# A spectral and matrix-root layer on one Trainium2 core: transfers and norms kept in the order of the source

## The chip, the cores and the metric

The kernel runs on one core of a Trainium2 chip. The core has five engines that matter here: TensorE (PE) multiplies matrices, and its weight loads have a row of their own (PEld); VectorE (DVE), ScalarE (ACT) and GpSimd (POOL) work elementwise; SyncE (SP) only issues transfers. Transfers (DMA) are issued here from SP's queue and from ACT's. Each engine has its own stream of instructions. The metric is the time of one execution in device microseconds (us), as the median of several runs; lower is better.

## What is computed

The input is 32 images of 32 channels of 128 x 128 values in float32. Two layers follow each other, each behind a group norm and each added to its input:

```
x = x + root(group_norm(x))     # per image and channel: Newton-Schulz iteration on A = the 128 x 128 plane
x = x + conv(group_norm(x))     # 2-D FFT, low modes mixed across channels by weights, inverse FFT

def root(A):                    # 5 steps
    norm = sqrt(sum(A * A));  Y = A / norm;  Z = I
    repeat 5:  T = 0.5 * (3 I - Z Y);  Y = Y T;  Z = T Z
    return Y * sqrt(norm)
```

The first layer takes nearly all of the matrix products: chains of 128 x 128 products for each of 1,024 planes. The second needs, for each image, products with small cosine and sine tables, a product over channels for each of the kept modes, and the way back.

## The kernel before, in words

**Sets and lanes.** Work of the first layer is cut into 256 sets; a set (b, g) is four channels of image b. `newton` (L296) is the chain of products of one set, written as a generator with twelve working steps and an end. Four lanes run four sets at a time, and one round of the main loop (L618 to L653) takes each lane one step on; lane i starts three rounds after lane i - 1. So a lane takes a new set every 13 rounds, and an image, eight sets, takes 26 rounds.

**Staging.** Before a set starts it is staged (`stage` L578, `staged` L260): POOL makes `x`, the normed transposed plane (L266, four instructions), ACT makes `b`, a scaled plane, in place (L274, four instructions), and POOL makes `r` from it (L282). Each time a lane takes a set, the next set is staged, and behind that the loads of the set two further on are issued from ACT's queue (`fetch` L254: L256 loads `b`, with 6 buffers, and L257 loads `xt`, with 14). Inside the chain, PE writes products to psum banks; DVE evacuates them as `v`, `w`, `q`, `t` (L237) and as the result `xt` (L317); ACT evacuates others as `y`, `m`, `mb`, `t` (L229, L231); POOL makes a second `r` from `mb` (L306).

**Statistics.** The norm of an image's first layer needs the statistics of the whole image, which `prep` (L156) makes for image b + 1 while image b is being staged: eight loads `xs` on SP (L163, two buffers), four statistics instructions on DVE for each (L171), and then a chain of small operations to `made[b]`. It takes one step a round.

**Forward.** Each finished pair of sets is transformed (`forward` L322): a product with a table (L326), a copy `sw` (L328), two stores of the result to the scratch tensor `mid` on SP (L330), statistics for the second norm (L332, L342), transposes and copies `u` (L337). After the fourth pair, `spectrum` (L350) ends with `spec` (L392) and its store to `xs` in DRAM (L403).

**Mode products and inverse.** The images fall into two groups, 28 and 4. When a group's spectra are stored, `mode_products` (L409) loads weights `wt` (L417) and spectra `xk` (L421), multiplies (L442), copies to `om` (L452, L454) and stores to `od` (L424), in 32 steps. Then `inverse` (L503) runs for each image: it loads `ob` (L474) and, for each half d of the image, two tiles `yt` of `mid` (L487, seven buffers of 512 KB), multiplies with tables (L524), copies `gt` (L534), multiplies again (L542), adds in place (L547), and stores the tile to `out` (L501). `store(lag)` keeps the last tile back for one step. In the source, the loads of the next half stand right behind the first tile's add of this half. Inverses of the first group are interleaved with the last sets of the first layer; what is left runs after the last set, in the `tail`, where some loads and stores go through ACT's queue.

**What sets the order.** The source above is traced once, and each engine gets its instructions from a scheduler. It keeps the dependencies of data and buffers. Apart from these it may put an instruction ahead of others that the source has before it on the same engine, when by the scheduler's own estimate of times its operands are ready sooner. At run time each queue is worked off in the order that the scheduler gave it.

Of the kernel before, what the change touches and what calls it, by code (L numbers as in the profile page):

```python
# [24 lines left out]
ALU = mybir.AluOpType  # L25
# [31 lines left out]
def conv_preact_kernel(  # L57
# [79 lines left out]
    def moments(st, tag):  # L137
# [15 lines left out]
        nc.vector.scalar_tensor_tensor(d, d, 64.0, f[:, :, :, 2], ALU.mult, ALU.add)  # L153
        return ms, nm, d

    def prep(b, made):  # L156

        st = small.tile([P, C, 6], F32, tag="a_st", name=f"a_st{b}")
        tiles = []

        def load(i):
            t = stp.tile([P, 4, P], F32, tag="xs", name=f"xs{b}_{i}")
            nc.sync.dma_start(out=t, in_=xt_in[b, :, 4 * i : 4 * i + 4, :])  # L163
            tiles.append(t)

        load(0)
        load(1)
        yield
        for i in range(C // 4):
            for c in range(4):  # L170
                nc.vector.bn_stats(st[:, 4 * i + c, :], tiles[i][:, c, :])  # L171
            if i + 2 < C // 4:
                load(i + 2)
            yield
        _, nm, d = moments(st, "a")
        q = small.tile([P, C], F32, tag="a_qs", name=f"a_qs{b}")
        nc.vector.tensor_reduce(
            q, d.rearrange("p g (c e) -> p (g c) e", e=2), AX.X, ALU.add
        )
        pq = bank()[:, 0, 0:C]  # L180
        nc.tensor.matmul(pq, avg_mean, q, start=True, stop=True)

        v = small.tile([P, C + G], F32, tag="a_v", name=f"a_v{b}")
        nc.vector.tensor_scalar_mul(v[:, 0:C], pq, -512 / (P * P))
        yield
        vg = small.tile([P, G], F32, tag="a_vg", name=f"a_vg{b}")
        nc.vector.tensor_reduce(
            vg, v[:, 0:C].rearrange("p (g c) -> p g c", c=2), AX.X, ALU.add
        )
        nc.vector.tensor_scalar(v[:, C:], vg, 0.5, EPS, ALU.mult, ALU.add)  # L190
        s = root(v, C + G, "a_r")
        inv = small.tile([P, C + G], F32, tag="a_inv", name=f"a_inv{b}")
        nc.vector.reciprocal(inv, s)
        yield

        sc = small.tile([P, C], F32, tag="a_sc", name=f"a_sc{b}")
        nc.vector.tensor_scalar_mul(sc, inv[:, 0:C], 1.0 / P)  # L197
        n = small.tile([P, G, 2], F32, tag="a_n", name=f"a_n{b}")
        nc.vector.tensor_tensor(
            n,  # L200
            s[:, 0:C].rearrange("p (g c) -> p g c", c=2),
            inv[:, C:, None].to_broadcast([P, G, 2]),
            ALU.mult,
        )
        nn = small.tile([P, C], F32, tag="a_nn", name=f"a_nn{b}")
        nc.vector.tensor_scalar_mul(
            nn, n.rearrange("p g c -> p (g c)"), P * (1.5 / EYE) ** 2
        )
        sn = root(nn, C, "a_t")

        scr = small.tile([P, C], F32, tag="a_scr", name=f"a_scr{b}")
        nc.vector.tensor_scalar_mul(scr, sc, QR * QS)
        off = small.tile([P, G, 2], F32, tag="a_off", name=f"a_off{b}")
        nc.vector.tensor_tensor(
            off,
            scr.rearrange("p (g c) -> p g c", c=2),
            nm[:, :, None].to_broadcast([P, G, 2]),
            ALU.mult,
        )
        made[b] = (nm, sc, sn, scr, off.rearrange("p g c -> p (g c)"))  # L220
        yield
# [31 lines left out]

    def fetch(b, g):  # L254
        xt, t = four("xt", 14), four("b", 6)
        nc.scalar.dma_start(out=t, in_=x[b, :, 4 * g : 4 * g + 4, :])  # L256
        nc.scalar.dma_start(out=xt, in_=xt_in[b, :, 4 * g : 4 * g + 4, :])  # L257
        raw[b, g] = xt, t

    def staged(b, g, nm, sc, sn, scr, off):  # L260

        chans = range(4 * g, 4 * g + 4)
        m = four("x", 4)
        xt, mb = raw.pop((b, g))
        for j, c in enumerate(chans):
            nc.gpsimd.tensor_scalar(  # L266
                m[:, j, :],
                xt[:, j, :],
                nm[:, c // 2 : c // 2 + 1],
                sc[:, c : c + 1],  # L270
                ALU.add,
                ALU.mult,
            )
            nc.scalar.activation(  # L274
                mb[:, j, :],
                mb[:, j, :],
                AF.Identity,
                bias=off[:, c : c + 1],
                scale=scr[:, c : c + 1],
            )  # L280
        r = four("r", 4)
        nc.gpsimd.tensor_tensor(r, mb, eye, ALU.add)  # L282
        return xt, m, mb, r
# [38 lines left out]
    def forward(b, q, u, st, pair):  # L322
# [4 lines left out]
        sw = sp.tile([P, 4, P], F32, tag="sw", name="sw", bufs=2)  # L327
        nc.scalar.copy(sw, ps)  # L328
        for i, xt in enumerate(pair):
            nc.sync.dma_start(out=mid[b][:, 8 * q + 4 * i : 8 * q + 4 * i + 4, :], in_=xt)  # L330
        for j in range(4):
            nc.vector.bn_stats(st[:, 8 * q + j, :], pair[0][:, j, :])  # L332
        yield
# [16 lines left out]
    def spectrum(b, u, st):  # L350
# [3 lines left out]
        for s in range(2):  # L354
# [45 lines left out]
        )  # L400
        yield
        i, j = where[b]
        nc.sync.dma_start(  # L403
            out=xs[i][:, :, j, :].rearrange("k p m -> p k m"),
            in_=spec.rearrange("p k q t -> p k (q t)"),
        )
        yield

    def mode_products(i):  # L409
# [3 lines left out]
        def load(step):  # L413
            kk, h = divmod(step, 2)
            for l4 in range(4):
                rows = slice(32 * l4, 32 * l4 + 32)
                (nc.scalar if tail and l4 % 2 else nc.sync).dma_start(  # L417
                    out=wts[step % len(wts)][rows, l4], in_=wk[kk, h, rows]
                )
            if not h:  # L420
                nc.sync.dma_start(out=xks[kk % len(xks)][:, 0:n, :], in_=xs[i][kk])  # L421

        def store(kk, om):
            nc.sync.dma_start(  # L424
                out=od[i][:, kk].rearrange("e q b x -> (q b) e x"),
                in_=om.rearrange("p (e o) l -> p e (o l)", e=2),
            )

        for step in range(len(wts)):
            load(step)  # L430
# [38 lines left out]
    def load_products(b):  # L469
        if b < B and b not in obs:  # L470
            g, n = where[b]
            pool, bufs = (ends[0], 4) if ends and last(b) else (inv, 2)
            obs[b] = pool.tile([P, 16, L], F32, tag="ob", name=f"ob{b}", bufs=bufs)
            nc.sync.dma_start(  # L474
                out=obs[b], in_=od[g][:, :, :, n].rearrange("e k q x -> (e k q) x")
            )

    def load_input(b, d):

        if (b, d) in yts:  # L480
            return
        yts[b, d] = []
        for e in range(2):
            o = 16 * e + 8 * d
            pool, tag, bufs = (ends[0], "late", 10) if ends and last(b) else (inv, "yt", 7)
            y = pool.tile([P, 8, P], F32, tag=tag, name=f"yt{b}_{o}", bufs=bufs)
            nc.sync.dma_start(out=y, in_=mid[b][:, o : o + 8, :])  # L487
            yts[b, d].append(y)

    def last(b):  # L490
# [7 lines left out]
    def store(lag):  # L498
        while len(stores) > lag:
            b, o, y = stores.pop(0)  # L500
            (nc.scalar if tail else nc.sync).dma_start(out=out[b, :, o : o + 8, :], in_=y)  # L501

    def inverse(b):  # L503

# [198 lines left out]
```

## Time and profile before

The time before is 3503.25 us, the median of 3 runs (3502.49 to 3504.72). The profiled execution has a span of 3507.2 us and a mean granted PE clock of 0.979.

| Engine | busy us | share of the span |
|---|---|---|
| PE | 3329.1 | 95% |
| PEld | 2980.6 | 85% |
| DVE | 2276.4 | 65% |
| ACT | 1461.1 | 42% |
| POOL | 1102.1 | 31% |

The transfers move 466.93 MB. The largest groups of issues are the loads `b`, `xt` and `xs` and the stores `mid` (256 issues each, 256 KB), the loads `yt` (128, 512 KB) and the stores `out` (128, 512 KB).

How to read the lines that follow: "L274" is line 274 of the kernel; `b<-in_x` names what is written and what is read, with buffer numbers left out; in a wait, the engine and line left of the arrow stood idle until what is right of it was done; "SPq" and "ACTq" are the queues that issue transfers. In a timeline a line gives the start, the duration, the engine, the line and the operation, how many instructions of the kind are merged, and in brackets the idle time of the engine just before and what ended it.

### The profile page before, as it was taken

What the parts mean: (1) busy time and instruction counts of PE and PEld (TensorE: products, weight loads), DVE (VectorE), ACT (ScalarE), POOL (GpSimd) and SP (SyncE); (2) the same over time, 40 slices, a digit from 0 to 9 for tenths busy, and PEclk for the clock granted to TensorE, in tenths of its full rate; (3) what the DMA queues carried; (4) which work ended last, traced back from release to release, by engine and by line L of the source; (5) the groups of instructions that cost most, each with busy time, mean ns of one, the idle gap of its engine ahead of it and who ended that gap; (6) DMA issues with size and microseconds to landing.
All of it is one profiled execution on the core that took longest, in us unless ns stands there. A gap on an engine that the chain in (4) does not pass through costs nothing.

```text
span 3507.2 us, 80642 instructions
## 1 busy us (share of the span) xinstructions
PE 3329.1 (95%) x31936; PEld 2980.6 (85%) x31936; DVE 2276.4 (65%) x6391; ACT 1461.1 (42%) x3025; POOL 1102.1 (31%) x1552
## 2 busy tenths in 40 slices
PE   5999999999999999999999999999999999899765
PEld 5999999999999999999999999999999886667433
DVE  6766666777776767676666666777676546556333
ACT  3444444444444444444444444444444443323111
POOL 4333333333333333333333333333333221111100
PEclk9999999999999999999999999999999999999877
DMA  5333223332333233322322333233323667867897
GB/s 186 125 110 96 88 88 94 97 97 91 97 97 96 92 96 98 93 93 90 95 90 86 94 97 97 91 97 97 95 94 100 201 208 250 268 226 247 281 317 271
DMA packets 281097, 466.93 MB, mean 133 GB/s; under 512 B 92176, under 2 KB 94224, under 8 KB 280720
## 3 DMA queue, kind: packets, MB, share of 16 engines
q1 hardware_dynamic: 198448, 303.40, 27.0%
q10 hardware_dynamic: 82272, 158.37, 14.1%
q8 instruction: 252, 4.13, 0.5%
q14 instruction: 125, 1.02, 0.1%
HBM read 302.28 MB, written 159.38 MB: 132 GB/s over the span
## 4 chain that ended last, share of the span: by engine, by line
PE 67%; DVE 15%; DMA 11%; issue 6%; POOL 1%; SPq 0%; ACT 0%; ACTq 0%; DVEq 0%; POOLq 0%
PE ps L243 51%; PE ps L249 9%; DMA xs<-in_xt 6%; PE ps L326 3%; DVE a_st L171 2%; PE ps L542 2%; DVE q L237 2%; DMA out<-yt 2%; DVE xt L317 2%; DVE w L237 1%; PE ps L442 1%; DMA yt<-mid 1%; DVE a_sc L197 1%; PE ps L524 1%; DVE b_st L342 1%
## 5 line engine op out<-in xcount | busy, mean ns | idle before, releaser
L306 POOL TENSOR_TENSOR r<-mb,eye 128x512 f32<-128x512 f32 x256 | 326.0, 1273 | 1562.4 <-ACT mb L231 1528.1
L266 POOL TENSOR_SCALAR x<-xt,a_nm,a_sc 128x128 f32<-128x128 f32 x1024 | 446.0, 453 | 599.7 <-PE ps L243 568.1
L243 PE MATMUL ps<-w,v 128*128 128x128 f32 x4096 | 549.1, 277 | 5.7 <-DVE w L237 5.5
L243 PE MATMUL ps<-y,q 128*128 128x128 f32 x4096 | 545.2, 276 | 0.0
L243 PEld LDWEIGHTS ps<-w,v 128*128 128x128 f32 x4096 | 500.2, 192 | 18.7 <-issue 8.7
L243 PEld LDWEIGHTS ps<-y,q 128*128 128x128 f32 x4096 | 500.2, 192 | 8.2 <-issue 8.1
L274 ACT ACTIVATE b<-b,a_off,a_scr 128x128 f32<-128x128 f32 x1024 | 430.0, 486 | 178.3 <-DMA b<-in_x 173.9
L237 DVE SCALAR_TENSOR_TENSOR w<-ps,r 128x512 f32<-128x512 f32 x512 | 350.3, 684 | 129.4 <-PE ps L249 124.3
L237 DVE SCALAR_TENSOR_TENSOR v<-ps,m 128x512 f32<-128x512 f32 x256 | 176.1, 688 | 355.4 <-PE ps L243 337.6
L229 ACT COPY y<-ps 128x512 f32<-128x512 f32 x512 | 299.9, 586 | 256.3 <-PE ps L243 248.5
L237 DVE SCALAR_TENSOR_TENSOR q<-ps,eye 128x512 f32<-128x512 f32 x512 | 347.5, 679 | 25.5 <-PE ps L243 9.9
L237 DVE SCALAR_TENSOR_TENSOR v<-ps,x 128x512 f32<-128x512 f32 x256 | 176.5, 689 | 254.1 <-PE ps L243 254.1
L282 POOL TENSOR_TENSOR r<-b,eye 128x512 f32<-128x512 f32 x256 | 326.2, 1275 | 0.0
L317 DVE SCALAR_TENSOR_TENSOR xt<-ps,a_t_s,xt 128x128 f32<-128x128 f32 x1024 | 292.7, 341 | 42.5 <-PE ps L243 42.4
L249 PE MATMUL ps<-ident,v 128*128 128x128 f32 x2048 | 317.9, 276 | 0.8 <-DVE v L237 0.8
L229 ACT COPY m<-ps 128x512 f32<-128x512 f32 x256 | 149.3, 583 | 401.1 <-PE ps L243 388.6
L243 PEld LDWEIGHTS ps<-m,q 128*128 128x128 f32 x2048 | 249.8, 192 | 70.4 <-DVE q L237 37.0
L243 PEld LDWEIGHTS ps<-x,q 128*128 128x128 f32 x2048 | 249.6, 192 | 57.1 <-DVE v L237 50.2
L547 DVE TENSOR_TENSOR yt<-ps,yt 128x512 f32<-128x512 f32 x256 | 164.5, 684 | 205.0 <-PE ps L542 190.2
L171 DVE BATCH_NORM_STATS2 a_st<-xs 128x6 f32<-128x128 f32 x1024 | 237.0, 278 | 84.6 <-DMA xs<-in_xt 84.0
L243 PE MATMUL ps<-m,q 128*128 128x128 f32 x2048 | 283.6, 281 | 7.4 <-DVE q L237 6.4
L243 PE MATMUL ps<-x,q 128*128 128x128 f32 x2048 | 282.5, 281 | 0.8 <-DVE q L237 0.8
(110 smaller groups left out, 5057.9 us busy)
## 6 DMA issues: line engine op xcount, KB each, us to landing
b<-in_x ACTq DMA_DIRECT2D x256, 256.0 KB, 2.9
xt<-in_xt ACTq DMA_DIRECT2D x256, 256.0 KB, 2.9
xs<-in_xt SPq DMA_DIRECT2D x256, 256.0 KB, 2.9
mid<-xt SPq DMA_DIRECT2D x256, 256.0 KB, 2.0
yt<-mid SPq DMA_DIRECT2D x128, 512.0 KB, 5.0
out<-yt SPq DMA_DIRECT2D x90, 512.0 KB, 5.6
out<-yt ACTq DMA_DIRECT2D x38, 512.0 KB, 6.8
od<-om SPq DMA_DIRECT2D x32, 512.0 KB, 3.5
```

The costliest lines, as they stand in the source:

```text
L171: nc.vector.bn_stats(st[:, 4 * i + c, :], tiles[i][:, c, :])
L229: nc.scalar.copy(t, ps)
L237: nc.vector.scalar_tensor_tensor(s, ps, f, t, ALU.mult, ALU.add)
L243: nc.tensor.matmul(ps[:, j, :], lhsT[:, j, :], rhs[:, j, :], start=True, stop=True)
L249: nc.tensor.transpose(ps[:, j, :], t[:, j, :], ident)
L266: nc.gpsimd.tensor_scalar(m[:, j, :], xt[:, j, :], nm[:, c // 2 : c // 2 + 1], sc[:, c : c + 1], ALU.add, ALU.mult,)
L274: nc.scalar.activation(mb[:, j, :], mb[:, j, :], AF.Identity, bias=off[:, c : c + 1], scale=scr[:, c : c + 1],)
L282: nc.gpsimd.tensor_tensor(r, mb, eye, ALU.add)
L306: nc.gpsimd.tensor_tensor(r, mb, eye, ALU.add)
L317: nc.vector.scalar_tensor_tensor(xt[:, j, :], ps[:, j, :], sn[:, c : c + 1], xt[:, j, :], ALU.mult, ALU.add)
L326: nc.tensor.matmul(ps[64 * i : 64 * i + 64], tab[:, T_FW], xt, start=True, stop=True)
L547: nc.vector.tensor_add(y, py[i], y)
```

## The change

Thirteen places are wrapped in `kept`, a helper of the framework. It adds an edge of order, without a wait, from the wrapped instruction to the one that the source has just before it on the same engine. The wrapped instruction then can't be issued ahead of anything that stood before it on that engine; instructions that are not wrapped still can be moved past it. Wrapped are all transfers of the loops (SP's and ACT's) and the two norms of a set (L266 on POOL and L274 on ACT). All operations, buffers and sizes stay as they were. It is for the case in which the scheduler takes an input as landed sooner than it lands, and puts an instruction that needs it ahead of work that could go.

```diff
         nc.vector.scalar_tensor_tensor(d, d, 64.0, f[:, :, :, 2], ALU.mult, ALU.add)
         return ms, nm, d
 
+    kept = tc.keep_in_program_order
+
     def prep(b, made):
 
         st = small.tile([P, C, 6], F32, tag="a_st", name=f"a_st{b}")
...
 
         def load(i):
             t = stp.tile([P, 4, P], F32, tag="xs", name=f"xs{b}_{i}")
-            nc.sync.dma_start(out=t, in_=xt_in[b, :, 4 * i : 4 * i + 4, :])
+            kept(nc.sync.dma_start(out=t, in_=xt_in[b, :, 4 * i : 4 * i + 4, :]))
             tiles.append(t)
 
         load(0)
...
 
     def fetch(b, g):
         xt, t = four("xt", 14), four("b", 6)
-        nc.scalar.dma_start(out=t, in_=x[b, :, 4 * g : 4 * g + 4, :])
-        nc.scalar.dma_start(out=xt, in_=xt_in[b, :, 4 * g : 4 * g + 4, :])
+        kept(nc.scalar.dma_start(out=t, in_=x[b, :, 4 * g : 4 * g + 4, :]))
+        kept(nc.scalar.dma_start(out=xt, in_=xt_in[b, :, 4 * g : 4 * g + 4, :]))
         raw[b, g] = xt, t
 
     def staged(b, g, nm, sc, sn, scr, off):
...
         m = four("x", 4)
         xt, mb = raw.pop((b, g))
         for j, c in enumerate(chans):
-            nc.gpsimd.tensor_scalar(
-                m[:, j, :],
-                xt[:, j, :],
-                nm[:, c // 2 : c // 2 + 1],
-                sc[:, c : c + 1],
-                ALU.add,
-                ALU.mult,
+            kept(
+                nc.gpsimd.tensor_scalar(
+                    m[:, j, :],
+                    xt[:, j, :],
+                    nm[:, c // 2 : c // 2 + 1],
+                    sc[:, c : c + 1],
+                    ALU.add,
+                    ALU.mult,
+                )
             )
-            nc.scalar.activation(
-                mb[:, j, :],
-                mb[:, j, :],
-                AF.Identity,
-                bias=off[:, c : c + 1],
-                scale=scr[:, c : c + 1],
+            kept(
+                nc.scalar.activation(
+                    mb[:, j, :],
+                    mb[:, j, :],
+                    AF.Identity,
+                    bias=off[:, c : c + 1],
+                    scale=scr[:, c : c + 1],
+                )
             )
         r = four("r", 4)
         nc.gpsimd.tensor_tensor(r, mb, eye, ALU.add)
...
         sw = sp.tile([P, 4, P], F32, tag="sw", name="sw", bufs=2)
         nc.scalar.copy(sw, ps)
         for i, xt in enumerate(pair):
-            nc.sync.dma_start(out=mid[b][:, 8 * q + 4 * i : 8 * q + 4 * i + 4, :], in_=xt)
+            kept(nc.sync.dma_start(out=mid[b][:, 8 * q + 4 * i : 8 * q + 4 * i + 4, :], in_=xt))
         for j in range(4):
             nc.vector.bn_stats(st[:, 8 * q + j, :], pair[0][:, j, :])
         yield
...
         )
         yield
         i, j = where[b]
-        nc.sync.dma_start(
+        kept(nc.sync.dma_start(
             out=xs[i][:, :, j, :].rearrange("k p m -> p k m"),
             in_=spec.rearrange("p k q t -> p k (q t)"),
-        )
+        ))
         yield
 
     def mode_products(i):
...
             kk, h = divmod(step, 2)
             for l4 in range(4):
                 rows = slice(32 * l4, 32 * l4 + 32)
-                (nc.scalar if tail and l4 % 2 else nc.sync).dma_start(
+                kept((nc.scalar if tail and l4 % 2 else nc.sync).dma_start(
                     out=wts[step % len(wts)][rows, l4], in_=wk[kk, h, rows]
-                )
+                ))
             if not h:
-                nc.sync.dma_start(out=xks[kk % len(xks)][:, 0:n, :], in_=xs[i][kk])
+                kept(nc.sync.dma_start(out=xks[kk % len(xks)][:, 0:n, :], in_=xs[i][kk]))
 
         def store(kk, om):
-            nc.sync.dma_start(
+            kept(nc.sync.dma_start(
                 out=od[i][:, kk].rearrange("e q b x -> (q b) e x"),
                 in_=om.rearrange("p (e o) l -> p e (o l)", e=2),
-            )
+            ))
 
         for step in range(len(wts)):
             load(step)
...
             g, n = where[b]
             pool, bufs = (ends[0], 4) if ends and last(b) else (inv, 2)
             obs[b] = pool.tile([P, 16, L], F32, tag="ob", name=f"ob{b}", bufs=bufs)
-            nc.sync.dma_start(
+            kept(nc.sync.dma_start(
                 out=obs[b], in_=od[g][:, :, :, n].rearrange("e k q x -> (e k q) x")
-            )
+            ))
 
     def load_input(b, d):
 
...
             o = 16 * e + 8 * d
             pool, tag, bufs = (ends[0], "late", 10) if ends and last(b) else (inv, "yt", 7)
             y = pool.tile([P, 8, P], F32, tag=tag, name=f"yt{b}_{o}", bufs=bufs)
-            nc.sync.dma_start(out=y, in_=mid[b][:, o : o + 8, :])
+            kept(nc.sync.dma_start(out=y, in_=mid[b][:, o : o + 8, :]))
             yts[b, d].append(y)
 
     def last(b):
...
     def store(lag):
         while len(stores) > lag:
             b, o, y = stores.pop(0)
-            (nc.scalar if tail else nc.sync).dma_start(out=out[b, :, o : o + 8, :], in_=y)
+            kept((nc.scalar if tail else nc.sync).dma_start(out=out[b, :, o : o + 8, :], in_=y))
 
     def inverse(b):
 
```

## The prediction

> **What bounds the kernel now.** I read the page's slices first, then the windows, then the waits of each stretch, then the timelines. The slices show three parts: a slow start, a long flat stretch, and an end in which TensorE (PE) empties while DMA fills.
>
> ```profile
> PE   5999999999999999999999999999999999899765
> PEclk9999999999999999999999999999999999999877
> DMA  5333223332333233322322333233323667867897
> ```
>
> The windows put numbers on them (columns: span, busy PE, PEld, DVE, ACT, POOL, granted clock, DMA share, GB/s).
>
> ```profile
> 0.00:100.00 100.00, 60.97 (x473) 57.61 (x474) 64.14 (x241) 36.17 (x80) 39.83 (x63) 1.00 0.58 185
> 1000.00:1500.00 500.00, 496.54 (x4230) 465.44 (x4226) 350.78 (x1032) 229.13 (x477) 181.40 (x256) 1.00 0.31 95
> 2900.00:3000.00 100.00, 88.70 (x1067) 62.75 (x1065) 58.85 (x138) 33.53 (x69) 16.96 (x24) 0.97 0.78 252
> 3000.00:3100.00 100.00, 87.06 (x1092) 62.57 (x1092) 48.78 (x96) 32.16 (x67) 16.97 (x24) 0.92 0.75 250
> 3300.00:3370.00 70.00, 41.51 (x514) 18.79 (x512) 20.38 (x42) 10.06 (x20) 8.83 (x6) 0.70 0.93 321
> ```
>
> From 100 to 2700 us PE is 99% busy, and the timeline shows its groups of eight matmuls back to back, one every 0.89 us (1522.24, 1523.13 and so on). Nothing off PE can shorten that. What can move lies in the start and after 2850 us, where the inverse transforms (L503 to L557) join the last sets. Waits from 2850 to 3230 (total us, times, longest):
>
> ```profile
> ACT b L274 <- DMA b<-in_x: 43.9, 10, 8.5
> PE ps L542 <- ACT gt L534: 18.0, 7, 5.2
> SPq L487 <- DMA out<-yt: 200.5, 67, 8.0
> ```
>
> The first two are one event. ScalarE (ACT) stands at a norm of a set (L274) whose input was issued at 2894.99; the copies `gt` behind it are late, and so is PE:
>
> ```profile
> 2902.16 1.26 ACT L274 ACTIVATE b<-b,a_off,a_scr 128x128 f32<-128x128 f32 x3 [8.54 <-DMA b<-in_x]
> 2904.86 2.08 PE L542 MATMUL ps<-gt,tab 64*128 64x512 f32 x4 [4.39 <-ACT gt L534]
> 2907.77 1.82 PE L243 MATMUL ps<-y,t 128*128 128x128 f32 x8
> ```
>
> Eight matmuls then take 1.82 us instead of 1.06: the clock fell too. The third wait is SyncE's queue (SP). Loads stand ahead of stores there: at 3244.10 a load goes, at 3244.47 two stores, then the queue stands 6 us at the next load, which needs a buffer that a store frees.
>
> ```profile
> 3244.10 0.32 SPq L487 DMA_DIRECT2D yt<-mid  x1
> 3244.47 0.91 SPq L501 DMA_DIRECT2D out<-yt  x2
> 3251.56 0.33 SPq L487 DMA_DIRECT2D yt<-mid  x1
> ```
>
> Stores that are ready wait behind it: image 18's third tile was added by 3232.7 and its store went at 3244.5.
>
> **What the Trainium skill says.** "TensorE: Matmul & The Clock Gate", Architectural detail, says that ACT's and VectorE's (DVE's) queues are strict FIFO; the 8.54 us above and the late copies behind it agree. The same page, Part 1, says that PE falls to half clock after an idle window of about 3.4 us; the 4.39 us gap and the 1.82 us group agree. "DMA: Bandwidth & Descriptors", Issuing engines are not separate DMA queues, says that all queues share the same 16 DMA engines, so reordering gives no bandwidth of its own; here loads land in 2.9 us (median) but in 7 to 12 us when many are out after 3300.
>
> **The change, part by part.** It adds no work. I compared the k-th instruction of each line in the trace with its place in the source. PE's order is already the source's up to 2690 us, except the small matmul L181. The pinned lines run early: L274 by 30 ACT instructions, L257 by 65, L256 by 12 (medians), L266 by 3 on GpSimd (POOL), and the statistics' loads L163 by some 25 SP instructions against the stores L330 around them (an image has 17 of both kinds). The copies on ACT, not pinned, keep their order among themselves.
>
> *Start, -10 us.* ACT now issues 20 input loads in the first 23 us and SP eight weight loads, between the eight loads of image 0's statistics; those land at 6.5 to 24.8. In source order only one set's two loads and the table accompany them. Estimate: first pair at about 6 and 7, then a pair every 3.85 us (0.33 issue + 2.5 landing, as in the quiet stretch from 29 on, + 0.87 statistics + 0.1), so the last statistics end at about 19.4 instead of 25.7: -6. Image 1's statistics no longer stand in the chain of small DVE operations (a 0.53 us wait and several pieces of 0.28): -1. POOL ran L266 of four sets ahead of the first L282, and the first `w` stood for it; in source order L282 follows four L266: -3.
>
> ```profile
> 41.13 0.69 DVE L237 SCALAR_TENSOR_TENSOR w<-ps,r 128x512 f32<-128x512 f32 x1 [3.41 <-POOL r L282]
> ```
>
> *Steady stretch, 0.* An image takes 93.4 us (the same store L330 of images 15 and 16 goes at 1505.02 and 1598.38), and eight sets on four lanes of 13 rounds are 26 rounds: 3.6 us a round. In source order a set's loads stand two stagings, 6.5 rounds or 23 us, ahead of its L274 and land in 2.9, so the 109.5 us of ACT waits for `b` between 200 and 2680 go; PE never felt them. New on ACT is a burst of 4 x 0.48 + 2 x 0.33 = 2.6 us per set. Behind it wait the copies of later lanes; a copy has a round of 3.6 us less 0.9 of matmuls and 0.6 of its own, so about 2 us of slack, and ACT is 46% busy. POOL's L266 and L282 (3.1 us) come a round or more ahead of the next L306. SP's L163 waits for the statistics two tiles back, L330 for adds a round old; behind each stand only loads due two rounds later. Bounds: 0 to +0.3 us per set.
>
> *2850 to 3230, -22 us.* PE's idle time there is 1.3 + 11.3 + 12.9 + 1.3 = 27 us, and the clock's shortfall 3 + 8 + 2 = 13 us, 40 in all. The waits for `b` vanish; those for late psum copies or an inverse's own latency stay. I take a little over half.
>
> *3230 to 3370, -22 us.* Stores go before loads, so the seven `yt` buffers come free sooner. Images 19 to 22 now take 18.1 us each (the same load L487 of images 19 and 23 goes at 3234.7 and 3307.1), for 4.25 MB of tiles; at the 321 GB/s of the next window that is 13.2 us: 4 x 4.9 = 20, of which I take 17, since other transfers share the rate. Then the last image's chain (copy `sw` 3313.7, `spec` 3349.3, its store landing after 12.4 us, 3.2 in the median) loses the weight issues and hoisted input loads ahead of it. But DMA is 93% busy there, and the ten hoisted tiles (5.2 MB, 16 us) only move into the next 95 us, which have 16% free: -5.
>
> *3370 to the end, 0.* SP is in source order there from 3403 on already.
>
> Sum: -10 - 22 - 22 = -54; 3503 - 54 = 3449 us.
>
> **The rivals.** (1) Hidden: the end is bound by bytes, and freed stores only crowd the loads. For it: 93% DMA share from 3300. Against: 75 to 78% before that. Then -10 - 11 = -21: 3482. (2) Slower: the ACT burst, or statistics that now come just in time, delay an evacuation in every round. For it: DVE is 70% busy and its statistics bunch into eight rounds an image. Against: they are bunched more densely now (a load every 1.5 to 2.5 us from 1555 on) and PE does not wait. At 0.3 us on 256 sets +77, less 54: 3526. (3) All of it: -12, -40, -40: 3411.
>
> **How the numbers follow.** Forecast 0.60, hidden 0.20, slower 0.12, all 0.08. The range runs from rival 3 to just above rival 1, 3411 to 3490, and leaves out rival 2. Within 0.2% (3496 to 3510) lie the edges of rivals 1 and 2, 0.04; slower 0.10; faster 0.86.
>
> **What would show it.** First matmul of a set at about 26 instead of 34 us; ACT waits for `b` near zero; PE 99% busy and clock 1.00 from 2900 to 3200; SP waits for `out` far under 200 us; stores within a few us of their adds. I am wrong if PE shows new waits for ACT or DVE between 200 and 2680, or if the inverses' adds (L547) wait for `yt`: those loads landed some 20 us ahead of use from 2900 to 3150 and will be issued one half-image, about 10 us, ahead of it, against 4 to 6 us to land.

## The result and the profile after

| | median us | range us | runs |
|---|---|---|---|
| before | 3502.87 | 3501.16 to 3504.72 | 4 |
| after | 3462.56 | 3458.04 to 3465.06 | 4 |

The ratio is 0.9883, with a 95% interval of 0.9866 to 0.9900: 40 us faster, where 54 us were forecast. The profiled executions lie further apart than the medians (3507.2 and 3456.3 us, 51.0). All stages below are read from one profiled execution of each kernel, so their sizes are good to some 5 to 10 us in the sum, and better where several kernels show the same.

The slices of the kernel after show how the end has changed: PE stays at nine tenths or more up to the 38th slice, where it had begun to give way at the 35th, and DMA is fuller.

```profile
PE   6999999999999999999999999999999999999955
PEclk9999999999999999999999999999999999999977
DMA  3323333333222232333333322233233568898997
```

Windows of the kernel after (columns as before: span, busy PE, PEld, DVE, ACT, POOL, granted clock, DMA share, GB/s). The last two are the stages that take the place of 3300 to 3370 us and of what followed.

```profile
0.00:100.00 100.00, 68.94 (x534) 65.78 (x534) 60.85 (x196) 32.86 (x69) 39.29 (x60) 0.98 0.35 114
1000.00:1500.00 500.00, 495.88 (x4225) 464.83 (x4224) 346.13 (x1004) 228.69 (x476) 183.37 (x258) 1.00 0.31 94
2900.00:3000.00 100.00, 99.24 (x1304) 70.98 (x1303) 62.89 (x150) 37.14 (x76) 20.12 (x29) 0.98 0.91 301
3000.00:3100.00 100.00, 99.56 (x1325) 71.41 (x1323) 62.99 (x125) 36.25 (x74) 20.43 (x28) 1.00 0.91 304
3230.00:3303.00 73.00, 55.21 (x884) 29.66 (x883) 38.36 (x82) 16.66 (x32) 8.90 (x6) 0.91 0.98 351
3303.00:3405.00 102.00, 62.44 (x1239) 43.78 (x1242) 19.56 (x30) 12.00 (x21) 0.00 (x0) 0.71 0.87 282
```

From 2900 to 3100 us PE went from 88 to 99% busy, as the forecast asked for. The waits of 2850 to 3230 us in the kernel after (total us, times, longest) have no line of ACT for `b` any more, and none of SP for `out`; SP now stands at the stores, until the add is done:

```profile
SPq L507 <- DVE yt L553: 142.4, 43, 7.5
ACT gt L540 <- PE ps L530: 66.4, 39, 5.3
```

At the start, DVE makes the first `w` at 32.07 instead of 41.13 us, and does not stand for `r`; what is just ahead of it are statistics of image 1, which were forecast to leave its way:

```profile
31.28 0.87 DVE L173 BATCH_NORM_STATS2 a_st<-xs 128x6 f32<-128x128 f32 x4 [0.49 <-DMA xs<-in_xt]
32.07 0.69 DVE L239 SCALAR_TENSOR_TENSOR w<-ps,r 128x512 f32<-128x512 f32 x1
```

Lines of the changed kernel are shifted: L163 is now L165, L256 and L257 are L258 and L259, L266 and L274 are L269 and L279 (their pins stand in L268 and L278), L330 is L336, L403 is L409, L417, L421 and L424 are L423, L427 and L430, L442 is L448, L474 is L480, L487 is L493, L501 is L507, L547 is L553.

**Where the time went.** The table compares the time of the same instruction in the traces: the end of set 31 (428.5 us before), the end of set 223 (2673.6), the first add of image 0's inverse (2880.2), of image 12's (3118.8), the first and the last matmul of the second group's mode products (3372.2 and 3458.3), and the end. Each cell is the change of one stage against the kernel before, in us; a minus is a gain. The kernels below "after" are the experiments.

| kernel, and what it keeps in order | to set 31 | sets 31 to 223 | to image 0 | images 0 to 12 | to modes of group 2 | modes of group 2 | rest | sum |
|---|---|---|---|---|---|---|---|---|
| after: all | -7.6 | +0.7 | +8.6 | -33.7 | -36.5 | +15.5 | +2.0 | -51.0 |
| e_act: ACT's loads, norms | -3.8 | -17.7 | +0.5 | -8.8 | +9.4 | -0.6 | -1.3 | -22.3 |
| e_sp: all but those | +1.6 | +17.0 | +11.5 | -11.9 | -36.3 | +18.9 | +0.9 | +1.7 |
| e_inv: ob, yt, out | +2.7 | -1.3 | +1.2 | -6.7 | -29.8 | +20.5 | +1.0 | -12.4 |
| e_actinv: both of these | -3.4 | -16.3 | -0.5 | -33.9 | -29.9 | +16.7 | +2.3 | -65.0 |
| e_norms: norms alone | -4.4 | -17.0 | +0.8 | -17.3 | +5.2 | -1.8 | +0.1 | -34.4 |
| e_fetch: ACT's loads alone | -3.6 | -2.8 | -0.6 | -9.6 | +6.9 | +1.6 | -0.3 | -8.4 |
| e_noxs: all but xs | -6.7 | -16.3 | +1.8 | -35.0 | -36.9 | +19.6 | -0.1 | -73.6 |
| e_nomp: all but wt, xk, od | -5.3 | +2.9 | +7.5 | -34.7 | -31.8 | +17.3 | +2.8 | -41.3 |
| e_actyt: e_act and yt | -5.9 | -19.8 | -1.1 | -34.7 | -30.6 | +11.7 | -0.6 | -81.0 |
| e_late: e_actinv, late yt free | -3.4 | -18.3 | -1.3 | -34.4 | -25.7 | +3.3 | -0.7 | -80.5 |
| e_ytlate: e_actyt, late yt free | -6.4 | -16.9 | -1.4 | -34.6 | -26.5 | +8.5 | -0.7 | -78.0 |
| e_noxslate: e_noxs, late yt free | -7.3 | -16.6 | +2.0 | -35.1 | -22.8 | +1.8 | +0.7 | -77.3 |

The whole change is thus a sum of large gains and of three losses (sets 31 to 223 next to e_act, the way to image 0, the modes of group 2), and the experiments are there to name the part behind each.

### The profile page after: what moved, and what is told of

Read it like the earlier page. It is cut to its first block, busy times and chain, and to the rows that moved or that the text cites. A ratio compares the mean times of both kernels' runs of the same rounds, so it can differ in the third digit from the quotient of the medians.

```text
span 3456.3 us, 80446 instructions
## 1 busy us (share of the span) xinstructions
PE 3315.2 (96%) x31936; PEld 2975.0 (86%) x31936; DVE 2264.4 (66%) x6391; ACT 1462.0 (42%) x3025; POOL 1108.4 (32%) x1552
## 3 DMA queue, kind: packets, MB, share of 16 engines
q10 hardware_dynamic: 82272, 158.37, 14.5%
## 4 chain that ended last, share of the span: by engine, by line
PE 83%; DMA 10%; DVE 5%; issue 1%; SPq 1%; ACTq 0%; ACT 0%; DVEq 0%
PE ps L245 62%; PE ps L251 10%; DMA xs<-in_xt 4%; PE ps L332 3%; PE ps L548 3%; PE ps L362 2%; PE ps L530 1%; DVE xt L323 1%; DVE a_st L173 1%; DMA xt<-in_xt 1%; DMA wt_late<-in_wk 1%; PE ps L448 1%; DMA yt<-mid 1%; DMA od<-om 1%; DMA out<-yt 1%; DVE q L239 1%
## 5 line engine op out<-in xcount | busy, mean ns | idle before, releaser
L269 POOL TENSOR_SCALAR x<-xt,a_nm,a_sc 128x128 f32<-128x128 f32 x1024 | 445.6, 449 | 21.7 <-DVE a_n L201 20.1
L279 ACT ACTIVATE b<-b,a_off,a_scr 128x128 f32<-128x128 f32 x1024 | 422.5, 486 | 1.8 <-DMA b<-in_x 1.6
L239 DVE SCALAR_TENSOR_TENSOR q<-ps,eye 128x512 f32<-128x512 f32 x512 | 347.4, 679 | 32.7 <-PE ps L245 19.6
L233 ACT ACTIVATE mb<-ps 128x512 f32<-128x512 f32 x256 | 154.0, 602 | 465.2 <-PE ps L251 463.2
L245 PE MATMUL ps<-m,q 128*128 128x128 f32 x2048 | 282.3, 280 | 16.2 <-DVE q L239 16.1
L245 PE MATMUL ps<-y,t 128*128 128x128 f32 x2048 | 280.2, 277 | 1.3 <-DVE t L239 1.2
```

The source lines that it names most:

```text
L233: nc.scalar.mul(t, ps, f)
L239: nc.vector.scalar_tensor_tensor(s, ps, f, t, ALU.mult, ALU.add)
L245: nc.tensor.matmul(ps[:, j, :], lhsT[:, j, :], rhs[:, j, :], start=True, stop=True)
L269: nc.gpsimd.tensor_scalar(m[:, j, :], xt[:, j, :], nm[:, c // 2 : c // 2 + 1], sc[:, c : c + 1], ALU.add, ALU.mult,)
L279: nc.scalar.activation(mb[:, j, :], mb[:, j, :], AF.Identity, bias=off[:, c : c + 1], scale=scr[:, c : c + 1],)
```

## Experiments

Every kernel is the changed one with some pins taken off. The helper is split in two, and a place that is to be left to the scheduler calls `free`:

```diff
-    kept = tc.keep_in_program_order
+    kept, free = tc.keep_in_program_order, lambda i: i
```

### One part of the change at a time

The working theory was that the two parts gain each for itself and add up: ACT's part (loads and norms) in the start and from 2850 us on, SP's part where stores stand behind loads. Of its rivals, S puts the whole gain on SP's order and A on ACT's.

**e_act**: only L258, L259, L268 and L278 are kept.

```diff
-            kept(nc.sync.dma_start(out=t, in_=xt_in[b, :, 4 * i : 4 * i + 4, :]))
+            free(nc.sync.dma_start(out=t, in_=xt_in[b, :, 4 * i : 4 * i + 4, :]))
...
-            kept(nc.sync.dma_start(out=y, in_=mid[b][:, o : o + 8, :]))
+            free(nc.sync.dma_start(out=y, in_=mid[b][:, o : o + 8, :]))
```

(and so at every other transfer of L336 to L507.)

> Only the set's two loads (L258, L259 in the changed kernel) and its norms (L268 on POOL, L278 on ACT) are kept in order; SP's queue stays free to be moved. Theory (two separate gains, ACT's queue in the start and from 2850 to 3230, SP's after that, less two losses of prefetching): the start gains 6 us, ACT's 44 us of waits for b from 2850 to 3230 go and with them some 25 us, stores still wait behind loads after 3230: about 3475. Rival S (SP's order is the whole gain, the waits for b only mirror crowded transfers): only the start moves, 3496. Rival A (ACT's order is the whole gain, the end is bound by bytes): as the whole change, 3462.

Measured: 3485.51 us, ratio 0.9944 (0.9921 to 0.9967).

**e_sp**: the opposite, every pin but those four places.

```diff
-        kept(nc.scalar.dma_start(out=t, in_=x[b, :, 4 * g : 4 * g + 4, :]))
-        kept(nc.scalar.dma_start(out=xt, in_=xt_in[b, :, 4 * g : 4 * g + 4, :]))
+        free(nc.scalar.dma_start(out=t, in_=x[b, :, 4 * g : 4 * g + 4, :]))
+        free(nc.scalar.dma_start(out=xt, in_=xt_in[b, :, 4 * g : 4 * g + 4, :]))
```

(and so at L268 and L278.)

> All transfers but the set's two loads are kept in order; those and the norms stay free. Theory: ACT's waits for b from 2850 to 3230 stay at some 40 us and so does PE's idle time there; stores go within a few us of their adds and the end gains some 35 us; the lost prefetching costs some 20: about 3488. Rival S: 3462. Rival A: no gain, 3503 or above.

Measured: 3508.97 us, ratio 1.0010 (0.9996 to 1.0024): no gain at all.

**e_inv**: only the transfers of the inverses, `ob` (L480), `yt` (L493) and `out` (L507), are kept; the diff is as for e_act.

> Only the inverse's transfers (ob, yt, out) are kept in order. Theory: the end gains some 35 us as above, the mode products keep their early weights, the first yt tiles are no longer early (+5): about 3478, with the waits for b from 2850 to 3230 as before. Rival S: 3462 or less. Rival A: 3503.

Measured: 3491.78 us, ratio 0.9967 (0.9958 to 0.9977).

**e_actinv**: the places of e_act and of e_inv together.

> The set's loads and norms and the inverse's transfers are kept in order; weights, spectra, statistics' loads and the stores to mid, xs and od stay free. Theory: both gains and only part of the losses, 3455, which is below the whole change. Rivals S and A: as the whole change, 3462.

Measured: 3442.46 us, ratio 0.9815 (0.9779 to 0.9852).

The kernel before had 3503.97 us beside these four. Alone the two parts gain 18 and 12 us, together 61. So the gains do not add, the theory falls, and both rivals with it. And e_actinv, which pins less than the change, is 20 us faster than the change.

### Why either part alone is worth little: two queues with one set of counters

From image 0 to image 12 (the fourth stage of the table) e_act gains 9 us, e_inv 7 and both 34. The trace of e_inv still has the waits for `b` (40.3 us in 10 times from 2850 to 3230 us, against 43.9 before). The one of e_act has hardly any left, but a new kind of stop on ACT. Its timeline at 3017 us:

```profile
3010.07 1.65 ACT L279 ACTIVATE b<-b,a_off,a_scr 128x128 f32<-128x128 f32 x4
3017.59 0.33 ACTq L258 DMA_DIRECT2D b<-in_x  x1
3019.53 0.34 ACTq L259 DMA_DIRECT2D xt<-in_xt  x1
3019.90 0.68 ACT L343 COPY u<-ps 128x256 f32<-128x256 f32 x2 [8.18 <-DMA yt<-mid]
```

Nothing of ACT runs from 3011.72 to 3019.90. It stands at the issue of two loads. Its releaser is named only at the next copy: a `yt` load on SP's queue, with which L259 shares no buffer. The landings in the trace say it more closely: L258 goes at 3017.59, a store to `mid` (issued by SP at 3011.49) had landed at 3017.57; L259 goes at 3019.53, the `yt` load of 3015.68 had landed at 3019.51. From 2850 to 3230 us 16 of the 24 loads of ACT in e_act waited, 37.9 us in all, and each of the 16 went 0.02 us after the landing of one of SP's transfers. In the changed kernel, e_actinv and e_norms no load waits in this way in that stretch.

The compiled program of e_act tells why. Its rows for these three instructions, with those of each one's waits that are for a transfer:

```
L258 DMACopy b<-in_x 128x512 [waits DMAHW0_49]
L259 DMACopy xt<-in_xt 128x512 [waits DMAHW7_49,DMAHW1_49]
L343 TensorCopy u_35347<-ps 128x64x4
```

`DMAHW0` to `DMAHW7` are eight completion counters. In this program they go round over the transfers of both queues, in the scheduler's joint order, and a transfer that takes a counter waits until the one that had it before has landed. So a load on ACT waits for a transfer on SP about eight places earlier. Where the scheduler put `yt` loads ahead of the stores that free their buffers, SP stands (in e_act 262.5 us in 71 times), the transfers behind land late, and ACT stands at its next load with every copy behind it. "TensorE: Matmul & The Clock Gate", Architectural detail, calls ScalarE's queue strict FIFO; here the standing instruction is not a computation but the issue of a transfer, and the cost is the 8.18 us above.

If that is the coupling, then of SP's transfers the `yt` loads alone must stand back. **e_actyt** is e_act with one line pinned:

```diff
-            free(nc.sync.dma_start(out=y, in_=mid[b][:, o : o + 8, :]))
+            kept(nc.sync.dma_start(out=y, in_=mid[b][:, o : o + 8, :]))
```

> ACT's loads (L258, L259), the norms (L268, L278) and of SP's transfers only the yt loads (L493) are pinned. Theory: pinning ACT's part alone gains only 18 us because SP stands at yt loads that the scheduler put ahead of the stores that free their buffers, and ACT's loads wait for SP's transfers to land (16 of 25 loads between 2850 and 3230 us, 37.9 us, each issued 0.02 us after such a landing). The yt loads alone are what has to stand back: about 3443 us, as with ob, yt and out pinned, ACT's waits ahead of its loads near 0 and SP's waits of L493 for out far under 262 us. Rival: the stores and ob loads must be pinned too, or the parts just add up (18 and a part of 12): 3470 us.

Measured: 3435.12 us (3428.42 to 3439.58), ratio 0.9808 (0.9789 to 0.9828), beside 3501.86 for the kernel before. One line more than e_act, and 50 us less. In the table 26 us are won between images 0 and 12 and 40 in the stage behind; 12 are lost again in the mode products. The rival at 3470 is out. ACT's waits ahead of its loads fall from 37.9 to 0.8 us, SP's waits of L493 for `out` from 262.5 to 0.7 us. The window of 3000 to 3100 us, first of e_act:

```profile
3000.00:3100.00 100.00, 89.17 (x1080) 63.50 (x1064) 50.83 (x100) 30.63 (x62) 16.40 (x24) 0.93 0.78 258
```

and of e_actyt:

```profile
3000.00:3100.00 100.00, 98.95 (x1329) 71.58 (x1329) 62.08 (x133) 36.15 (x73) 20.08 (x29) 1.00 0.87 292
```

What this doesn't settle: e_actyt frees both SP and, through it, ACT. A kernel in which ACT's loads have counters of their own, with SP still standing, was not tried.

### The long stretch: the norms gain 17 us, the statistics loads lose them again

Sets 31 to 223 were forecast at zero. The whole change does come out at +0.7 there, but e_act at -17.7 and e_sp at +17.0. Three kernels take this apart.

**e_norms** keeps only the norms, **e_fetch** only ACT's two loads.

```diff
-            kept(nc.sync.dma_start(out=t, in_=xt_in[b, :, 4 * i : 4 * i + 4, :]))
+            free(nc.sync.dma_start(out=t, in_=xt_in[b, :, 4 * i : 4 * i + 4, :]))
...
-        kept(nc.scalar.dma_start(out=t, in_=x[b, :, 4 * g : 4 * g + 4, :]))
-        kept(nc.scalar.dma_start(out=xt, in_=xt_in[b, :, 4 * g : 4 * g + 4, :]))
+        free(nc.scalar.dma_start(out=t, in_=x[b, :, 4 * g : 4 * g + 4, :]))
+        free(nc.scalar.dma_start(out=xt, in_=xt_in[b, :, 4 * g : 4 * g + 4, :]))
```

(this for e_norms, and all of L336 to L507 free in both; e_fetch has `free` at L268 and L278 instead of L258 and L259.)

> Only the norms of a set (L268 on GpSimd, L278 on ACT) are pinned, no transfer. Theory: in the kernel before, a norm of ACT stands 3.1 us (median) behind the issue of its own load, so that ACT waits for each load to land; pinning the norms alone undoes that, and the loads then go even earlier. So set 223 comes about as early as with all of ACT's part pinned (21 us), less what the start loses by the many early loads (4 us), and ACT's loads, which go far ahead of their norms, leave ACT free of waits for b between 2850 and 3230 us: 3485 us, or less. Rival: it is the loads that must be held back, since early ones stand on ACT until a buffer of b is free; then ACT waits there and the time is about 3503 us.

> Only the input loads of a set on ACT (L258, L259) are pinned, no norm. Theory: the norms are still put right behind the loads (4 instructions of ACT lie between them in the middle of the run), so ACT still waits for b some 2 us per set; nothing of the steady gain comes, and only the start is shorter: 3497 us. Rival: the loads are what matters, 3485 us as with loads and norms pinned.

Measured, beside 3504.01 for the kernel before: e_norms 3476.64 us, ratio 0.9928 (0.9908 to 0.9948); e_fetch 3496.38 us, ratio 0.9977 (0.9969 to 0.9986). Both rivals fall. Of the 17.7 us, 17.0 are the norms' alone. ACT's timeline of the middle of the run shows what is wrong with their place in the kernel before:

```profile
1511.80 0.33 ACTq L256 DMA_DIRECT2D b<-in_x  x1
1512.19 0.65 ACT L337 COPY u<-ps 128x256 f32<-128x256 f32 x2 [0.74 <-PE ps L249]
1514.63 0.49 ACT L274 ACTIVATE b<-b,a_off,a_scr 128x128 f32<-128x128 f32 x1 [1.79 <-DMA b<-in_x]
```

The norm stands two short copies behind the issue of its own load: 3.2 us from issue to norm in the median of all sets, and 0.0 from landing to norm. So ACT's queue often waits out the landing of the load (97.5 us in 84 times from 430 to 2680 us). With the change it is 23.6 us from issue to norm. In e_fetch the wait stays (152.0 us at L279); in e_norms there is none (its loads go far ahead, and 70.5 us of waits at loads of `xt` take their place without a loss that shows).

But PE does not show these waits as its own. In the kernel before it waits 15.0 us from 430 to 2680 us, and 0.3 of them for ACT; and e_fetch, where ACT waits longer for `b`, is 2.8 us ahead in this stage. What PE did feel is in part the other norm, GpSimd's (L266, now L269), which is pinned together with ACT's. From set 31 to set 223 PE and DVE take their instructions in the same order, tile for tile, before and in e_norms, so the two can be compared place by place. The place of the first norm's statistics, before:

```profile
1543.74 1.74 POOL L266 TENSOR_SCALAR x<-xt,a_nm,a_sc 128x128 f32<-128x128 f32 x4 [1.30 <-PE ps L243]
1544.30 0.40 DVE L152 TENSOR_TENSOR a_d<-a_d 128x64 f32<-128x64 f32 x1
1544.73 0.41 DVE L153 SCALAR_TENSOR_TENSOR a_d<-a_d,a_st 128x64 f32<-128x64 f32 x1
1545.92 0.30 PE L181 MATMUL ps<-a_qs,avg_mean 128*128 128x32 f32 x1 [0.17 <-DVE a_qs L177]
```

and in e_norms:

```profile
1528.34 1.73 POOL L269 TENSOR_SCALAR x<-xt,a_nm,a_sc 128x128 f32<-128x128 f32 x4
1531.50 0.23 DVE L152 TENSOR_TENSOR a_d<-a_d 128x64 f32<-128x64 f32 x1
1531.76 0.24 DVE L153 SCALAR_TENSOR_TENSOR a_d<-a_d,a_st 128x64 f32<-128x64 f32 x1
1532.87 0.30 PE L183 MATMUL ps<-a_qs,avg_mean 128*128 128x32 f32 x1
```

Before, GpSimd's norms run over this chain of DVE in every image; L152 and L153 take 0.39 and 0.42 us (medians), and PE stands for `a_qs` each time. In e_norms GpSimd is done by then, the two take 0.23 and 0.25 us, and PE does not stand. ACT's norm runs beside them there, from 1531.36 us on, and does not slow them. The same split goes through all fourteen kernels: PE waits for `a_qs` 23 or 24 times in the four whose norms are free (before, e_sp, e_inv, e_fetch), and never in the other ten. In e_norms this place is 0.27 us shorter per image, which over 24 images is 6 of the 17 us. Another 0.32 us per image (8 us) are won at the first groups of an image, where PE often stood for a `q` that DVE made late behind statistics. How much of that is due to ACT's norm and how much to GpSimd's stays open, since no kernel pins one without the other.

**e_noxs** is the whole change with only the statistics loads free:

```diff
-            kept(nc.sync.dma_start(out=t, in_=xt_in[b, :, 4 * i : 4 * i + 4, :]))
+            free(nc.sync.dma_start(out=t, in_=xt_in[b, :, 4 * i : 4 * i + 4, :]))
```

> The whole change, but the statistics loads of the first norm (L165) are left to the scheduler. Theory: the whole change gains some 18 us between sets 31 and 223 by the pinned norms and input loads and loses as much again because L165 now comes just in time, so that DVE's statistics and with them the evacuations behind them come late. Then this kernel is at about 3446 us, DVE's waits for xs between 430 and 2680 us fall from 133.5 to about 50 us, PE's waits there from 18.7 to about 4 us, and set 223 ends some 16 us sooner against the whole change. Rival: the loss comes from the pinned stores to mid and xs in DRAM (L336, L409), which stay pinned here; then 3462 us and no difference at set 223.

Measured: 3434.87 us (3431.81 to 3437.90), ratio 0.9803 (0.9788 to 0.9819). Set 223 ends 16.1 us sooner than in the changed kernel, as expected, and the total is another 11 us better than expected. The waits from 430 to 2680 us, in the changed kernel:

```profile
DVE a_st L173 <- DMA xs<-in_xt: 133.5, 119, 2.8
PE ps L245 <- DVE q L239: 14.4, 23, 0.7
```

and in e_noxs:

```profile
DVE a_st L173 <- DMA xs<-in_xt: 48.9, 69, 3.0
PE ps L245 <- DVE q L239: 2.1, 4, 1.4
```

DVE stands at statistics whose tile has not landed, `q` behind them is late, and PE stands for `q` about once per image. How much this is shows the window of 430 to 2660 us, in the order before, after, e_noxs:

```profile
430.00:2660.00 2230.00, 2214.06 (x18835) 2073.88 (x18834) 1561.28 (x4547) 1016.67 (x2125) 810.23 (x1146) 1.00 0.30 94
```
```profile
430.00:2660.00 2230.00, 2210.80 (x18830) 2072.55 (x18828) 1551.91 (x4542) 1015.19 (x2117) 814.67 (x1145) 1.00 0.31 94
```
```profile
430.00:2660.00 2230.00, 2224.11 (x18971) 2088.80 (x18970) 1557.22 (x4586) 1021.02 (x2137) 819.82 (x1153) 1.00 0.29 95
```

PE's idle time is 15.9, 19.2 and 5.9 us of 2230. And e_noxs gets through 136 more matmuls than the kernel before in the same time; at 2230 / 18835 = 0.118 us each that is 16 us, the stage's gain. Of it 10 us are idle time that went; the other 6 are matmuls that follow each other more closely without a gap that the profile counts, and their cause stays open.

### The way to image 0

The changed kernel loses 8.6 us between set 223 and the first add of the inverses, e_act nothing. **e_nomp** tests the first suspect, weights and spectra that are no longer fetched ahead:

```diff
-                kept((nc.scalar if tail and l4 % 2 else nc.sync).dma_start(
+                free((nc.scalar if tail and l4 % 2 else nc.sync).dma_start(
```

(and so at L427 and L430.)

> The whole change, but the transfers of the mode products (wt L423, xk L427, od L430) are left to the scheduler. Theory: the 8 us that the whole change loses between 2674 and 2880 us, beside the kernel with only ACT's part pinned, are weights and spectra that are no longer fetched ahead; here they come back, and of the 17 us lost in the last mode products a few: 3452 us. Rival: the first yt tiles, which stay pinned here, are what comes late at 2880 us, and the last mode products stay as long: 3462 us.

Measured: 3468.50 us, ratio 0.9896 (0.9879 to 0.9913), with the loss still there (+7.5). The theory falls. Its rival is near the number, but e_noxs shows that the `yt` pin isn't the cause either: it is there too, and the loss is 1.8. It is the statistics loads again. Six of the last image's eight are issued from 2678 to 2692 us in the kernel before and from 2655 to 2669 in e_noxs (the other two earlier still), but all eight from 2863 to 2894 in the changed kernel, in the middle of the first inverses' loads. SP's timeline there, changed kernel:

```profile
2870.58 1.10 SPq L165 DMA_DIRECT2D xs<-in_xt  x2
2872.19 0.33 SPq L480 DMA_DIRECT2D ob<-od  x1
2872.56 0.91 SPq L493 DMA_DIRECT2D yt<-mid  x2
```

PE is busy 34.8 of the 40 us from 2860 to 2900 there, at a granted clock of 0.93, and in e_noxs 38.2 of the 40 us from 2840 to 2880 at 1.00, which hold about the same work (the first add comes 22.9 us earlier there).

### The last mode products: tiles that moved in among the weights

The mode products of group 2 take 86.1 us before and 101.6 after. Their window in the kernel before:

```profile
3372.00:3458.00 86.00, 54.58 (x1243) 41.28 (x1244) 20.39 (x31) 12.18 (x22) 0.00 (x0) 0.75 0.85 281
```

The kernel after moves 28.80 MB in this stage where the kernel before moved 24.18, and has 16 loads `yt` in it instead of 5. Both run at 281 to 282 GB/s. The 4.62 MB more at 282 GB/s are 16.4 us, and the stage is 15.5 us longer. **e_late** is e_actinv with the ten late `yt` tiles (images 28 to 30) left to the scheduler, which puts them back ahead of the weights:

```diff
-            kept(nc.sync.dma_start(out=y, in_=mid[b][:, o : o + 8, :]))
+            (free if tag == "late" else kept)(nc.sync.dma_start(out=y, in_=mid[b][:, o : o + 8, :]))
```

> ACT's part and ob, yt, out pinned as in the fastest kernel so far (3442 us), but the ten late yt tiles of images 28 to 30 are left to the scheduler, which then issues them before and early in the last mode products instead of among their weights. Theory: these tiles are what makes the last mode products 17 us longer (103 instead of 86 us); the 5.2 MB go into a stretch that is 93% full, so that some 7 of the 17 us are paid there: 3432 us. Rival, bytes only: the tiles cost the same wherever they go, 3442 us.

Measured: 3429.80 us (3428.55 to 3431.59), ratio 0.9789 (0.9775 to 0.9804), the fastest of all. The stage gets 13.4 us shorter than in e_actinv, and 4.2 are paid in the stage ahead of it. So the rival, bytes only, falls: the tiles cost less ahead of the mode products, where the DMA share is 0.95, than among them. Nor are bytes all of the 13.4 us. In this stage e_late moves 26.3 MB and e_actinv 28.3; 2.0 MB are 7 us at 282 GB/s. For the rest the rate is higher, 289 instead of 275 GB/s. That weights no longer stand behind tiles in SP's queue would explain it, but no run shows it alone.

**e_ytlate** and **e_noxslate** make the same edit in e_actyt and in e_noxs.

> ACT's loads and norms and the yt loads are pinned, but for the ten late yt tiles of images 28 to 30, which are left to the scheduler. Theory: the gain of pinning only the yt loads of SP (3435 us) and the gain of leaving the late tiles free (12.7 us, measured with ob and out pinned too) have different places and add up: 3423 us. Rival: both are the same relief of the last 150 us, where the transfers fill 84 to 93% of the time: 3430 us.

> The whole change without the pin on the statistics loads (L165) and without the pin on the ten late yt tiles. Theory as for the kernel with only ACT's part and yt pinned: 3435 - 12 = 3423 us. Rival: with the weights pinned, the late tiles go in among other transfers and hold up the weights that follow them in the queue: 3435 us.

Measured: 3432.99 us (3429.41 to 3435.37) and 3432.30 us (3431.74 to 3433.74), ratios 0.9800 (0.9782 to 0.9817) and 0.9799 (0.9783 to 0.9815). Freeing the late tiles gains 2 and 3 us here, not 12, and even these are not clear of the spread of the runs. Both results lie by their rivals. For e_noxslate that holds of the number only: its mode products are 18 us shorter than those of e_noxs, and the stage ahead of them is 14 us longer. From image 12 to the end the table has -23 for e_late, -19 for e_ytlate and -20 for e_noxslate. Five kernels with different pins end between 3430 and 3435 us. It may be that one and the same limit is reached in several ways. The bytes alone are not shown to be it: from image 12 on the five move 109 to 110 MB at 294 to 299 GB/s, where the changed kernel reached 351 for 73 us. What the limit is stays open.

## Why the prediction was right, and where it was not

The time fell in the range, 14 us above the number. The steps, by the profiled executions:

- **Start, -10: -7.5** at the end of set 3 (102.6 to 95.1 us). The largest term was good: the last statistics of image 0 end at 19.4 us, as worked out (though the parts named for a pair of tiles add up to 3.80 us and not to 3.85). What failed is the term of -1 for statistics of image 1 that would leave DVE's way; the lines of the start above show four of them right ahead of `w`.
- **Steady stretch, 0: +0.7**, for the wrong reason. The step said "PE 99% busy" and "Nothing off PE can shorten that". PE's idle share was 0.7% of 2230 us, 15.9 us, more than the whole step for the start; in e_norms 6.0 are left of it, and the stage is 17.0 us shorter. "PE never felt them", of ACT's waits for `b`, is borne out as far as the trace shows: 0.3 us of PE's waits are for ACT. What the step left out is GpSimd. It took L266 only as a producer that is early enough, and put at nothing that L266 runs over DVE's statistics; that alone was 6 us. And the statement that "behind each stand only loads due two rounds later" left out DVE: L165 just in time made it wait 133.5 us for `xs`, and cost 16 us. This was rival 2's mechanism. Its 0.3 us per set was too much: 16 us on 192 sets are 0.08.
- **2850 to 3230, -22.** The step was right in what goes: no ACT wait for `b`, PE at 99%, clock 1.00 from 3000 on. Its size from image 0 to image 12 is -33.7: of the 40 us of idle time and lost clock that were counted from 2850 to 3230 us most came back, not "a little over half" (from 2850 to 3230 us 7.0 us of idle time are left, and 5 of lost clock). Taken with the +8.6 of the way to image 0, which no step foresaw, the two make -25.
- **But the reason given for it was half.** The step laid the gain on the norms alone, and the next on stores before loads, and summed. e_norms gets -17.3 in this stage, e_act -8.8, e_inv -6.7, both together -33.9. Loads of ACT wait for SP's transfers, which the prediction had no step for.
- **3230 to 3370, -22: -36.5.** Stores now go when their tile is ready: image 18's third tile was added by 3200.1 us and its store went at 3200.1, where it had waited 12 us. The stretch runs at 351 GB/s and a DMA share of 0.98 from 3230 to 3303 us; the step had reckoned with 321.
- **3370 to the end, 0: +17.5.** This is the largest miss. The step had seen the ten tiles, "5.2 MB, 16 us", and let them "move into the next 95 us, which have 16% free". The free share was not to be had: the stage runs at 281 GB/s before and 282 after, with 5 and with 16 tiles in it, and they cost their whole 16 us. In e_late, put back ahead of this stage, they cost 4.

The last two misses (-14.5 and +17.5) nearly cancel, since the tiles that left the one stage came into the other; so do the two opposite halves of the steady stretch. The sum was better than its terms: that the time came within 14 us of the forecast is in part luck. Of the signs named ahead, those of right came (no wait for `b`, PE full, SP's waits for `out` gone, stores at their adds, and the first matmul of a set at 28.0 us where about 26 was named). So did one of wrong: PE's waits for DVE between 200 and 2680 us, 21.1 us where there were 16.0. The other, adds that wait for `yt`, did not come: none between 2850 and 3230 us, and 4.7 us after that, where the kernel before had 10.1.

## What to carry to other kernels

Read a long flat stretch by its idle microseconds, not by its share: 0.7% of it was 16 us, more than the whole forecast for the start. Look there also at engines that nobody waits for: where GpSimd's work falls decided how long DVE's took. When an order is pinned, pin what must not run ahead (here the norms, and the `yt` loads that need buffers which later stores free) and leave free what gains by running ahead (the statistics loads, the late tiles): five places pinned gave 67 us, all thirteen 40. And test parts of such a change together as well as alone, since a stall in one queue can hold another through the counters of their transfers.

## What the runs showed of the hardware

- Two issuing queues can stand for each other's transfers. In this compiled program, with eight completion counters for both, 16 of 24 loads on ACT in e_act (2850 to 3230 us) went 0.02 us after a landing on SP, having waited 37.9 us. "DMA: Bandwidth & Descriptors", Issuing engines are not separate DMA queues, says that a second issuing engine saves only the time to start a transfer; here it also brought the first one's stalls with it.
- A DMA share below 1 did not turn out to be room. In the mode products (weights in loads of 64 KB, tiles and results in transfers of 512 KB) four kernels (before, after, e_actinv, e_late) stayed at 275 to 289 GB/s at shares of 0.83 to 0.87. In the changed kernel the same engines moved 351 GB/s at 0.98 from 3230 to 3303 us, where most transfers are tiles of 512 KB. The same page's Specifications give about 358 GB/s as a core's limit to HBM; the measurement goes above that, with 372 GB/s from 3237 to 3287 us, so the figure was no ceiling for this core.
- GpSimd and DVE are not free of each other. Two small DVE operations (128 x 64) took 0.39 and 0.42 us while GpSimd's norms ran and 0.23 and 0.25 us while they did not, in the medians of the kernel before and of e_norms; a third (L149) took 0.26 and 0.25 us.
